# Four graph layers on 128 small graphs: two more columns in the H B^-1 H' matmuls, and the first weights loaded in smaller pieces in another order

## The chip, the core and the metric

The kernel runs on one core of a Trainium2 chip. The metric is the device time of one execution in microseconds (us), where smaller is better. Matmuls run on TensorE (PE in the profile, with its weight loads as PEld), elementwise work on VectorE (DVE), ScalarE (ACT) and GpSimd (POOL). SyncE (SP) issues every DMA, in one queue and in program order.

## What is computed

There are 128 graphs of 64 nodes with 512 features (x), each with a 64x64 weighted adjacency matrix (adj, many entries zero). Four layers follow each other, and each one is `x = layernorm(x + layer(x))`:

```
layer 0:  s = (x @ w0) @ a0;  A = exp(leaky(8*tanh((s_i + s_j)/8))) * adj, rows normalised
          to the sum of adj's row;  out = A @ x @ w0
layer 1:  attention: adj * exp(q k^T), rows normalised, times v   (weights Wq, Wk, Wv)
layer 2:  a graph-wide softmax of q_i . (sum_j adj_ij k_j), times v   (Wqk, Wv)
layer 3:  two hypergraph convolutions with relu and layernorm between them:
          H = (adj != 0);  w = first row of adj
          Dn_i = sum_e H_ie w_e;  Be_e = number of nodes in e
          conv(x, W) = Dn^-1 H Be^-1 H^T (x @ W^T) + b
```

For this case two things matter. The first is the matrix `G = H Be^-1 H^T` (64x64 for each graph), with the sums that go with it: Dn, the number of edges of each node, and the row sums of adj. The second is that layer 1 and layer 2 need only the product of their q and k weights, so the kernel forms `M1 = Wq^T Wk` and `M2` once, at the start.

## The kernel before, in words

**Tiling.** The 8192 nodes are 64 tiles of 128 rows, two graphs in a tile. Two tiles make a group: there are 32 groups (NG), and `run(g)` (line 986) issues all four layers of one. Two groups make a chunk: there are 16 chunks, and `prepare_chunk(c)` (line 680) makes for four tiles at a time what depends on adj alone. All data is float32, and TensorE takes a float32 matmul as two passes, so one matmul of the program is two MATMUL rows in the trace (the transposes are one).

**Products.** A 256x512 by 512x512 product is done by `seven_products` in Strassen-Winograd form, with seven block products in place of eight. The weights stand in DRAM as prepared blocks (b11, t1, b21, ... "w", "v", "3a", "3b") and are streamed for every group into a pool of eight buffers called ring. Group 0 uses the blocks of w0 straight from where they were made (`first_use`); group 1 is the first that reads them back (DMA ring<-w).

**TensorE modes.** Matmuls over all 128 rows and columns are "whole". Work on single graphs runs on 64x64 quarters of the array (mode "quarters"; in the profile 64*64) or on halves of its columns ("columns", 128*64).

**Order of the work.** Nothing is issued in source order. Every operation is recorded with an engine, an estimated cost, a key (its due time) and the buffers it touches. `Order.run` (line 140) then plays a list schedule with these costs, and `choose` (line 122) weighs whether TensorE stays in its mode or turns. The resulting order on each engine is fixed by dependencies ("pinned", line 1153), so the profile has nearly all instructions on one line, L1159, and tiles must be used to tell them apart. A DMA's recorded size sets how long the plan takes the link to be busy; for x and adj, `load` (line 338) records 2*128*1024 bytes in both cases. SP has at most eight DMAs under way: the ninth waits for the first to land.

**Start.** Wq and Wk are loaded in halves of 256 rows with key -12 (lines 418 to 425), then w0, a0, x of group 0 and adj of chunk 0. `gram` (line 553) forms M1: for each of four column blocks c it takes a PSUM bank and adds four steps of k (128 rows of weight each), two steps for each operation. M2 follows from Wqk in the same way. The row dots of w0 with a0 give u0 = w0 a0, from which s comes.

**G of a chunk.** hA is H, bh is H Be^-1 (written by POOL), and w is a small tile of its own (128 x 4 x 2), whose first column ACT fills with the first row of adj and whose second column is one. Line 708 issues the matmuls of a chunk as quarters:

```
quarters_of(N, lambda g: N * g, hA, lambda i: bh.t[:, i])
quarters_of(1, lambda g: P + 3 * g, turned, lambda i: ones)
quarters_of(2, lambda g: P + 3 * g + 1, hA, lambda i: w.t[:, i])
```

Each call is eight matmuls (2 x 2 x 2), with 64, one and two columns. The first gives G, the second the row sums of adj, and the third Dn and the edge counts. The first and the third have the same weights, hA. They write into the same two banks, from which ACT copies G into gm and DVE copies the sums.

Of the kernel before, what the change touches and what calls it, by code (L numbers as in the profile page):

```python
# [16 lines left out]
P = 128  # L17
B, N, D, DH = 128, 64, 512, 1024
T = B * N // P
GT = 2  # L20
# [222 lines left out]
def w_pe(n, times=1):  # L243
    return times * 2 * max(112, n * 27 // 32)
# [15 lines left out]
def kernel(  # L260
# [34 lines left out]
    def kind(name, n, *shape, space=None):  # L295
        kinds[name] = [(space or sbuf).tile([P, *shape], FP, name=f"{name}{i}") for i in range(n)]
# [4 lines left out]
    kind("h", 2, GT, DH)  # L301
    kind("k2", 2, D)
    kind("adj", 10, CT, N)
    kind("kept", 12, CT, N)
    kind("k1", 2, CT, N)
    kind("e", 7, GT, N)
    kind("w", 2, CT, 2)
    kind("col", 40, 16)
    kind("bank", 8, D, space=psum)
    kinds["product"] = [None] * 3  # L310
# [27 lines left out]
    def load(b, src, view=None):  # L338
        dma(2 * P * 1024, [], [b], lambda: view(b.t) if view else b.t, lambda: src)

    NOW = 100.0

# [2 lines left out]
    make_identity(nc, ident)  # L345
    ones = sb("ones", 1)
    nc.vector.memset(ones, 1.0)
    for t_ in kinds["w"]:
        nc.vector.memset(t_, 1.0)
    mhalf = sb("mhalf", GT)  # L350
    nc.vector.memset(mhalf, -0.5)
# [29 lines left out]
    xs, adjs, turned_adjs, prepared = {}, {}, {}, {}  # L381

    def load_x(g):
        order.key = BASE[g] - 6.0 if g else -11.0
        xs[g] = Buf("x", 4)
        load(xs[g], x_g[g])

    def load_adj(c):
        order.key = BASE[GC * c] - 7.0 if c else -10.5
        adjs[c] = Buf("adj")  # L390
        load(adjs[c], adjT[:, ts(c, CT * N)], lambda t_: t_.rearrange("p t i -> p (t i)"))

        turned = turned_adjs[c] = Buf("adj", 2 * GT)
        for t in range(GT):
            for h in range(2):
                dma(P * 256, [], [turned[2 * t + h]],
                    lambda t=t, h=h: turned.t[ts(t, N)].rearrange("p (g h) i -> p g h i", h=2)[:, :, h],
                    lambda t=t, h=h: adjT_c[c, t][:, :, h])
# [16 lines left out]
    def rows_of(b, cols):  # L415
        return b.t.rearrange("p (c o) -> p c o", o=cols)

    order.key = -12.0
    wq1_raw, wk1_raw = [], []
    for h in range(2):  # L420
        for made, w in ((wq1_raw, wq1), (wk1_raw, wk1)):
            b = Buf("k4", 2)
            order.add("SP", 500, [], [b], lambda b=b, h=h, w=w: nc.sync.dma_start(
                out=rows_of(b, D), in_=w.rearrange("(h c p) o -> h p c o", h=2, p=P)[h]), size=4 * P * 1024)
            made.append(b)
    order.key = -11.5
    w0_raw = raw(w0, 2, "ring")
    a0_b = Buf("k2")
    dma(P * 2048, [], [a0_b], lambda: a0_b.t,
        lambda: bass.AP(tensor=a0.tensor, offset=a0.offset, ap=[[0, P], [1, D]]))  # L430
    load_x(0)
    load_adj(0)
    mask_c = plain_in("mask_c", mask, T)
    order.key = -10.0
# [115 lines left out]

    def gram(name, left, right):

        m = const(sb(name, len(USE), 2, D // 2), 2 * len(USE))
        place = {k: i for i, k in enumerate(USE)}
        place["b12"] = place["t3"]

        def emit(ps, c, h):
            for k in (2 * h, 2 * h + 1):  # L560
                nc.tensor.matmul(ps.t, rows_of(left[h], D)[:, k % 2, ts(c, P)], rows_of(right[h], D)[:, k % 2],
                                 start=(k == 0), stop=(k == KC - 1))
# [38 lines left out]


    wqk_h = wqk2.rearrange("(h o) i -> h o i", h=2)
    order.key = -9.5
    wq2_raw, wk2_raw = raw(wqk_h[0], 2), raw(wqk_h[1], 2)
# [74 lines left out]
    def prepare_chunk(c):  # L680
        order.key = BASE[GC * c] - 3.0 if c else 0.5
        adj, turned = adjs[c], turned_adjs[c]
        m = mask_c.t[:, ts(c, CT)]
        hA, bh, am = (Buf("kept") for _ in range(3))
# [12 lines left out]

        ps = [Buf("bank") for _ in range(2)]
        gm, sums = Buf("kept"), Buf("col")

        def quarters_of(n, at, left, right):
            for g in range(CT // 2):
                for h, (cols, _) in enumerate(halves):
                    for t, (rows, _) in enumerate(halves):
                        nc.tensor.matmul(ps[t].t[cols, at(g) : at(g) + n], left.t[rows, 2 * g + h], right(2 * g + h)[rows],
                                         start=True, stop=True)

        def emit_g():
            quarters_of(N, lambda g: N * g, hA, lambda i: bh.t[:, i])
            quarters_of(1, lambda g: P + 3 * g, turned, lambda i: ones)  # L710
            quarters_of(2, lambda g: P + 3 * g + 1, hA, lambda i: w.t[:, i])

        pe(720, [turned, hA, bh, w], [*ps, gm], emit_g, mode="quarters", matmuls=40)
        for t in range(2):
            act(P, [ps[t]], [gm], lambda t=t: nc.scalar.copy(
                gm.t.rearrange("p (g t) i -> p t g i", t=2)[:, t], ps[t].t[:, :P].rearrange("p (g i) -> p g i", i=N)), NOW)
            dve(6, [ps[t]], [sums], lambda t=t: nc.vector.tensor_copy(
                sums.t[:, : 3 * CT].rearrange("p (k g t) -> p t g k", t=2, k=3)[:, t],
                ps[t].t[:, P : P + 6].rearrange("p (g k) -> p g k", k=3)), NOW)
        radj = sums  # L720
        dn, n_edges = (slice(CT * k, CT * (k + 1)) for k in (1, 2))
# [18 lines left out]
        prepared[c] = adj, turned, gm, am, radj, g1, dc, dh  # L740


    KEYS = ("11", "12", "21", "22")
# [242 lines left out]
    def run(g):  # L986
# [3 lines left out]

        step(0)
        xt = xs.pop(g)
        adj, turned, gm, am, radj, g1, dc, dh = prepared[g // GC]
# [29 lines left out]
        seven_products(*left, first_use["w0"] if g == 0 else streamed("w0"), *scaled_into(at_x, radj, own, D // 2))  # L1023
        layer_norm(xt)


# [203 lines left out]
```

## Time and profile before

| | us |
|---|---|
| median of 3 runs | 2177.75 |
| lowest and highest | 2177.24, 2178.48 |
| the profiled execution's own time | 2177.52 |
| its span in the trace (first to last instruction) | 2175.7 |
| TensorE busy in the span | 2153.9 |
| VectorE, ScalarE, GpSimd busy | 1557.7, 856.3, 386.1 |
| moved by DMA | 476.36 MB, mean 219 GB/s |

The span is what the trace covers; the execution's own time has 1.8 us more. The page of the profile gives busy times and the chain of work that ended last. The timeline merges instructions of one kind that follow each other into a row of start, length, what it is and how many; matmuls are pipelined and their ends are modelled, so the cost of a block is read from its start to the start of the next one, not from its length. The view of waits totals the idle time of an engine by what ended it. The view by windows gives the busy time, the granted TensorE clock (PEclk, 1.00 is full) and the DMA rate of a stretch.

### The profile page before, as it was taken

What the parts mean: (1) busy time and instruction counts of PE and PEld (TensorE: products, weight loads), DVE (VectorE), ACT (ScalarE), POOL (GpSimd) and SP (SyncE); (2) the same over time, 40 slices, a digit from 0 to 9 for tenths busy, and PEclk for the clock granted to TensorE, in tenths of its full rate; (3) what the DMA queues carried; (4) which work ended last, traced back from release to release, by engine and by line L of the source; (5) the groups of instructions that cost most, each with busy time, mean ns of one, the idle gap of its engine ahead of it and who ended that gap; (6) DMA issues with size and microseconds to landing.
All of it is one profiled execution on the core that took longest, in us unless ns stands there. A gap on an engine that the chain in (4) does not pass through costs nothing.

```text
span 2175.7 us, 51913 instructions
## 1 busy us (share of the span) xinstructions
PE 2153.9 (99%) x21085; PEld 1720.9 (79%) x21085; DVE 1557.7 (72%) x3967; ACT 856.3 (39%) x1812; POOL 386.1 (18%) x399
## 2 busy tenths in 40 slices
PE   8999999999999999999999999999999999999998
PEld 4887787877887788888878877878887888878866
DVE  5777767677777777777777776777777777766675
ACT  2435343343433433343443434434334333343433
POOL 1113021021201222111222111212012221012120
PEclk9999999999999999999999999999999999999999
DMA  9676668667665667666666666676656666655475
GB/s 299 229 252 242 206 206 280 220 215 238 215 219 198 208 219 236 218 200 207 211 227 218 220 206 206 205 239 216 217 196 213 224 220 223 204 192 204 159 255 196
DMA packets 174302, 476.36 MB, mean 219 GB/s; under 512 B 35760, under 2 KB 45296, under 8 KB 174064
## 3 DMA queue, kind: packets, MB, share of 16 engines
q1 hardware_dynamic: 174064, 473.05, 65.7%
q8 instruction: 166, 2.72, 0.5%
q14 instruction: 72, 0.59, 0.1%
HBM read 443.33 MB, written 29.66 MB: 217 GB/s over the span
## 4 chain that ended last, share of the span: by engine, by line
PE 98%; DMA 1%; DVE 0%; ACT 0%; issue 0%; SPq 0%; DVEq 0%; ACTq 0%
PE bank L1159 98%; DMA ring<-w 0%; DMA x<-in_x_dram 0%; DVE k L1159 0%; DMA k<-in_wk_dram 0%; ACT x L1159 0%; ACT k L1159 0%; DVE col L1159 0%; DVE x L1159 0%; SPq L1159 0%; DVE h L1159 0%; ACT u_b L1159 0%; ACT e L1159 0%; DVEq L1159 0%; ACTq L1159 0%
## 5 line engine op out<-in xcount | busy, mean ns | idle before, releaser
L1159 PE MATMUL bank<-ring,k 128*128 128x256 f32 (+1 forms) x3968 | 1039.9, 410 | 3.0 <-ACT k L1159 1.9
L1159 PEld LDWEIGHTS bank<-ring,k 128*128 128x128 f32 x3968 | 728.3, 190 | 207.2 <-issue 113.7
L1159 ACT COPY k<-bank 128x512 f32<-128x512 f32 (+1 forms) x640 | 304.2, 503 | 646.6 <-PE bank L1159 558.4
L1159 DVE SCALAR_TENSOR_TENSOR x<-bank,col,x 128x256 f32<-128x256 f32 (+1 forms) x832 | 400.3, 500 | 194.0 <-PE bank L1159 183.5
L1159 PEld LDWEIGHTS bank<-k,m 128*128 128x128 f32 x3584 | 428.6, 192 | 29.1 <-issue 17.2
L1159 PE MATMUL bank<-k,m 128*128 128x128 f32 x3584 | 437.8, 275 | 0.6 <-ACT k L1159 0.5
L1159 PE MATMUL bank<-ring,h 128*128 128x256 f32 (+1 forms) x1408 | 412.7, 439 | 0.0
L1159 POOL TENSOR_TENSOR col<-col,mhalf 128x2 f32<-128x2 f32 (+1 forms) x161 | 111.6, 693 | 1462.8 <-DVE col L1159 1171.8
L1159 PEld LDWEIGHTS bank<-ring,h 128*128 128x128 f32 x1408 | 259.1, 190 | 81.5 <-issue 55.0
L1159 DVE TENSOR_TENSOR k<-bank,k 128x256 f32<-128x256 f32 x384 | 154.0, 422 | 142.2 <-PE bank L1159 136.8
L1159 ACT ACTIVATE x<-x,col,col 128x512 f32<-128x512 f32 x256 | 195.9, 810 | 148.7 <-DVE col L1159 146.4
L1159 DVE BATCH_NORM_STATS2 col<-x 128x6 f32<-128x512 f32 x256 | 174.9, 689 | 6.3 <-DVE x L1159 0.5
L1159 DVE SCALAR_TENSOR_TENSOR h<-bank,col,b3a_b 128x512 f32<-128x512 f32 x128 | 95.7, 748 | 63.7 <-PE bank L1159 63.0
L1159 ACT ACTIVATE k<-bank,u_c 128x128 f32<-128x128 f32 x256 | 80.4, 365 | 133.5 <-PE bank L1159 130.2
L1159 DVE TENSOR_TENSOR k<-k 128x256 f32<-128x256 f32 x226 | 107.3, 475 | 32.5 <-ACT k L1159 32.0
L1159 ACT ACTIVATE h<-h 128x512 f32<-128x512 f32 x128 | 80.3, 630 | 110.8 <-DVE h L1159 110.7
L1159 ACT ACTIVATE h<-h,col,col 128x512 f32<-128x512 f32 x128 | 95.6, 805 | 68.1 <-DVE col L1159 68.0
L1159 PEld LDWEIGHTS bank<-k,k 128*64 128x64 f32 (+1 forms) x2112 | 77.6, 140 | 51.7 <-DVE k L1159 24.5
L1159 PE MATMUL bank<-k,k 128*64 128x64 f32 (+1 forms) x2112 | 106.6, 238 | 6.8 <-DMA k<-in_wk_dram 6.2
L1159 DVE SCALAR_TENSOR_TENSOR h<-bank,col,h 128x512 f32<-128x512 f32 x128 | 93.1, 747 | 20.8 <-PE bank L1159 19.6
L1159 POOL TENSOR_TENSOR k<-k,b3b_b 128x512 f32<-128x512 f32 x64 | 81.4, 1271 | 134.0 <-DVE h L1159 65.0
L1159 POOL TENSOR_TENSOR x<-x,bv_b 128x512 f32<-128x512 f32 x64 | 81.2, 1272 | 76.5 <-PE bank L1159 57.6
(98 smaller groups left out, 1511.2 us busy)
## 6 DMA issues: line engine op xcount, KB each, us to landing
ring<-3a SPq DMA_DIRECT2D x224, 512.0 KB, 4.5
ring<-3b SPq DMA_DIRECT2D x224, 512.0 KB, 4.5
ring<-v SPq DMA_DIRECT2D x189, 512.0 KB, 3.9
ring<-w SPq DMA_DIRECT2D x93, 512.0 KB, 3.4
x<-in_x_dram SPq DMA_DIRECT2D x32, 512.0 KB, 4.5
ring<-v SPq DMA_DIRECT2D x63, 256.0 KB, 3.7
out_dram<-x SPq DMA_DIRECT2D x31, 512.0 KB, 3.4
ring<-w SPq DMA_DIRECT2D x31, 256.0 KB, 4.1
```

The costliest lines, as they stand in the source:

```text
L1159: made = f(*args, **kwargs)
```

## The change

In the chunk's matmuls, the two columns of w move into bh, which becomes 66 columns wide. The third call of `quarters_of` is gone; G, Dn and the edge counts come out of one call with 66 columns. A graph's results now lie 67 columns apart in the bank, with the row sum of adj as the last one. The plan's cost of this operation goes from 720 to 400 ns and its count of matmuls from 40 to 16.

At the start, Wq and Wk come in pieces of 128 rows, a0 and the halves of w0 are put between them, then x of group 0; x of group 1 gets an earlier key, and the turned parts of adj of chunk 0 a later one. `gram` takes a number of steps: M1 takes one k at a time over all four banks, M2 two at a time. The sizes that the plan assumes for x and adj are the real ones. The two halves of Wqk are loaded in turn (q, k, q, k). The pool "kept" has nine buffers, with two of the kind bh beside it.

```
-    kind("kept", 12, CT, N)
+    kind("kept", 9, CT, N)
+    kind("bh", 2, CT, N + 2)
-    kind("w", 2, CT, 2)
...
-        order.key = BASE[g] - 6.0 if g else -11.0
+        order.key = (-11.0, -10.3)[g] if g < 2 else BASE[g] - 6.0
-        load(xs[g], x_g[g])
+        load(xs[g], x_g[g], P * GT * D * 4)
...
+        order.key += 0.0 if c else 0.6
...
     order.key = -12.0
-    for h in range(2):
-        for made, w in ((wq1_raw, wq1), (wk1_raw, wk1)):
-            b = Buf("k4", 2)
-            order.add("SP", 500, [], [b], lambda b=b, h=h, w=w: nc.sync.dma_start(
-                out=rows_of(b, D), in_=w.rearrange("(h c p) o -> h p c o", h=2, p=P)[h]), size=4 * P * 1024)
-            made.append(b)
-    order.key = -11.5
-    w0_raw = raw(w0, 2, "ring")
-    a0_b = Buf("k2")
-    dma(P * 2048, [], [a0_b], ...)
-    load_x(0)
+    for k in range(KC):
+        load_rows(wq1_raw, wq1, k)
+        load_rows(wk1_raw, wk1, k)
+        if k == 0:
+            dma(P * 2048, [], [a0_b], ...)
+            load_half(w0_raw, w0, 0)
+        if k == 1:
+            load_half(w0_raw, w0, 1)
+            load_x(0)
+            order.key = -12.0
...
-    def gram(name, left, right):
+    def gram(name, left, right, steps):
...
-        for c in range(KC):
-            ps = Buf("bank")
-            for h in range(2):
-                pe(w_pe(D, KC // 2), [left[h], right[h]], [ps], lambda ps=ps, c=c, h=h: emit(ps, c, h))
+        banks = [Buf("bank") for _ in range(KC)]
+        for ks in (range(i, i + KC // steps) for i in range(0, KC, KC // steps)):
+            for c in range(KC):
+                pe(w_pe(D, len(ks)), [b[k // 2][k % 2] for k in ks for b in (left, right)], [banks[c]],
+                   lambda c=c, ks=ks: emit(banks[c], c, ks))
...
-    m1 = gram("m1", wq1_raw, wk1_raw)
+    m1 = gram("m1", wq1_raw, wk1_raw, KC)
-    m2 = gram("m2", wq2_raw, wk2_raw)
+    m2 = gram("m2", wq2_raw, wk2_raw, KC // 2)
...
-        pool(W, [hA, be], [bh], lambda: nc.gpsimd.tensor_mul(bh.t, hA.t, per_tile(be.t[:, :CT])))
-        w = Buf("w")
-        act(CT, [turned], [w], lambda: nc.scalar.copy(w.t[:, :, 0:1], turned.t[:, :, 0:1]))
+        pool(W, [hA, be], [bh[0]], lambda: nc.gpsimd.tensor_mul(bh.t[:, :, :N], hA.t, per_tile(be.t[:, :CT])))
+        act(CT, [turned], [bh[1]], lambda: nc.scalar.copy(bh.t[:, :, N : N + 1], turned.t[:, :, 0:1]))
...
-            quarters_of(N, lambda g: N * g, hA, lambda i: bh.t[:, i])
-            quarters_of(1, lambda g: P + 3 * g, turned, lambda i: ones)
-            quarters_of(2, lambda g: P + 3 * g + 1, hA, lambda i: w.t[:, i])
-        pe(720, [turned, hA, bh, w], [*ps, gm], emit_g, mode="quarters", matmuls=40)
+            quarters_of(N + 2, lambda g: (N + 3) * g, hA, lambda i: bh.t[:, i])
+            quarters_of(1, lambda g: (N + 3) * g + N + 2, turned, lambda i: ones)
+        pe(400, [turned, hA, bh], [*ps, gm], emit_g, mode="quarters", matmuls=16)
```

More of the change, by code (lines that the diff above doesn't have):

```diff
@@ L336, in dma, with load @@
         order.add("SP", 500, reads, writes, lambda: nc.sync.dma_start(out=out(), in_=in_()), size=size)
-    def load(b, src, view=None):
-        dma(2 * P * 1024, [], [b], lambda: view(b.t) if view else b.t, lambda: src)
+    def load(b, src, size, view=None):
+        dma(size, [], [b], lambda: view(b.t) if view else b.t, lambda: src)
     NOW = 100.0
@@ L347 @@
     nc.vector.memset(ones, 1.0)
-    for t_ in kinds["w"]:
+    for t_ in kinds["bh"]:
         nc.vector.memset(t_, 1.0)
@@ L390, in load_adj @@
         adjs[c] = Buf("adj")
-        load(adjs[c], adjT[:, ts(c, CT * N)], lambda t_: t_.rearrange("p t i -> p (t i)"))
+        load(adjs[c], adjT[:, ts(c, CT * N)], P * CT * N * 4, lambda t_: t_.rearrange("p t i -> p (t i)"))
         turned = turned_adjs[c] = Buf("adj", 2 * GT)
+        order.key += 0.0 if c else 0.6
         for t in range(GT):
@@ L416, in rows_of, with load_rows, load_half @@
         return b.t.rearrange("p (c o) -> p c o", o=cols)
-    order.key = -12.0
-    wq1_raw, wk1_raw = [], []
-    for h in range(2):
-        for made, w in ((wq1_raw, wq1), (wk1_raw, wk1)):
-            b = Buf("k4", 2)
-            order.add("SP", 500, [], [b], lambda b=b, h=h, w=w: nc.sync.dma_start(
-                out=rows_of(b, D), in_=w.rearrange("(h c p) o -> h p c o", h=2, p=P)[h]), size=4 * P * 1024)
-            made.append(b)
-    order.key = -11.5
-    w0_raw = raw(w0, 2, "ring")
-    a0_b = Buf("k2")
-    dma(P * 2048, [], [a0_b], lambda: a0_b.t,
-        lambda: bass.AP(tensor=a0.tensor, offset=a0.offset, ap=[[0, P], [1, D]]))
-    load_x(0)
+    wq1_raw, wk1_raw = ([Buf("k4", 2) for _ in range(2)] for _ in range(2))
+    w0_raw = [Buf("ring", 2) for _ in range(2)]
+    a0_b = Buf("k2")
+    def load_rows(b, w, k):
+        order.add("SP", 500, [], [b[k // 2][k % 2]], lambda: nc.sync.dma_start(
+            out=rows_of(b[k // 2], D)[:, k % 2], in_=w[ts(k, P)]), size=P * D * 4)
+    def load_half(b, w, h):
+        order.add("SP", 500, [], [b[h]], lambda: nc.sync.dma_start(
+            out=rows_of(b[h], D), in_=w.rearrange("(h c p) o -> h p c o", h=2, p=P)[h]), size=P * PIECE * 4)
+    order.key = -12.0
+    for k in range(KC):
+        load_rows(wq1_raw, wq1, k)
+        load_rows(wk1_raw, wk1, k)
+        if k == 0:
+            dma(P * 2048, [], [a0_b], lambda: a0_b.t,
+                lambda: bass.AP(tensor=a0.tensor, offset=a0.offset, ap=[[0, P], [1, D]]))
+            load_half(w0_raw, w0, 0)
[3 more added lines that the diff above has]
+            order.key = -12.0
     load_adj(0)
@@ L557, in gram, with emit @@
         place["b12"] = place["t3"]
-        def emit(ps, c, h):
-            for k in (2 * h, 2 * h + 1):
-                nc.tensor.matmul(ps.t, rows_of(left[h], D)[:, k % 2, ts(c, P)], rows_of(right[h], D)[:, k % 2],
+        def emit(ps, c, ks):
+            for k in ks:
+                nc.tensor.matmul(ps.t, rows_of(left[k // 2], D)[:, k % 2, ts(c, P)], rows_of(right[k // 2], D)[:, k % 2],
                                  start=(k == 0), stop=(k == KC - 1))
+        banks = [Buf("bank") for _ in range(KC)]
[3 more added lines that the diff above has]
+                   lambda c=c, ks=ks: emit(banks[c], c, ks))
         for c in range(KC):
-            ps = Buf("bank")
-            for h in range(2):
-                pe(w_pe(D, KC // 2), [left[h], right[h]], [ps], lambda ps=ps, c=c, h=h: emit(ps, c, h))
+            ps = banks[c]
             for i in range(2):
@@ L603 @@
     wqk_h = wqk2.rearrange("(h o) i -> h o i", h=2)
+    wq2_raw, wk2_raw = ([Buf("k4", 2) for _ in range(2)] for _ in range(2))
     order.key = -9.5
-    wq2_raw, wk2_raw = raw(wqk_h[0], 2), raw(wqk_h[1], 2)
+    for h in range(2):
+        load_half(wq2_raw, wqk_h[0], h)
+        load_half(wk2_raw, wqk_h[1], h)
     order.key = 3.0
-    m2 = gram("m2", wq2_raw, wk2_raw)
+    m2 = gram("m2", wq2_raw, wk2_raw, KC // 2)
     order.key = 6.0
@@ L683, in prepare_chunk @@
         m = mask_c.t[:, ts(c, CT)]
-        hA, bh, am = (Buf("kept") for _ in range(3))
+        hA, bh, am = Buf("kept"), Buf("bh", 2), Buf("kept")
         be = Buf("col")
@@ L708, in emit_g, with per_g @@
         def emit_g():
-            quarters_of(N, lambda g: N * g, hA, lambda i: bh.t[:, i])
-            quarters_of(1, lambda g: P + 3 * g, turned, lambda i: ones)
-            quarters_of(2, lambda g: P + 3 * g + 1, hA, lambda i: w.t[:, i])
-        pe(720, [turned, hA, bh, w], [*ps, gm], emit_g, mode="quarters", matmuls=40)
+            quarters_of(N + 2, lambda g: (N + 3) * g, hA, lambda i: bh.t[:, i])
+            quarters_of(1, lambda g: (N + 3) * g + N + 2, turned, lambda i: ones)
+        pe(400, [turned, hA, bh], [*ps, gm], emit_g, mode="quarters", matmuls=16)
+        def per_g(t):
+            return ps[t].t[:, : CT // 2 * (N + 3)].rearrange("p (g k) -> p g k", k=N + 3)
         for t in range(2):
             act(P, [ps[t]], [gm], lambda t=t: nc.scalar.copy(
-                gm.t.rearrange("p (g t) i -> p t g i", t=2)[:, t], ps[t].t[:, :P].rearrange("p (g i) -> p g i", i=N)), NOW)
+                gm.t.rearrange("p (g t) i -> p t g i", t=2)[:, t], per_g(t)[:, :, :N]), NOW)
             dve(6, [ps[t]], [sums], lambda t=t: nc.vector.tensor_copy(
                 sums.t[:, : 3 * CT].rearrange("p (k g t) -> p t g k", t=2, k=3)[:, t],
-                ps[t].t[:, P : P + 6].rearrange("p (g k) -> p g k", k=3)), NOW)
-        radj = sums
-        dn, n_edges = (slice(CT * k, CT * (k + 1)) for k in (1, 2))
+                per_g(t)[:, :, N:]), NOW)
+        dn, n_edges, radj = (slice(CT * k, CT * (k + 1)) for k in range(3))
         g1, dc, dh = Buf("col"), Buf("col"), Buf("col")
@@ L739, in prepare_chunk @@
         dve(W, [am, mr], [am], lambda: nc.vector.tensor_mul(am.t, am.t, mr.t))
-        prepared[c] = adj, turned, gm, am, radj, g1, dc, dh
+        prepared[c] = adj, turned, gm, am, sums, g1, dc, dh
     KEYS = ("11", "12", "21", "22")
@@ L992, in run @@
         xt = xs.pop(g)
-        adj, turned, gm, am, radj, g1, dc, dh = prepared[g // GC]
+        adj, turned, gm, am, sums, g1, dc, dh = prepared[g // GC]
         own = slice(g % GC * GT, g % GC * GT + GT)
@@ L1022, in run @@
         step(2)
-        seven_products(*left, first_use["w0"] if g == 0 else streamed("w0"), *scaled_into(at_x, radj, own, D // 2))
+        seven_products(*left, first_use["w0"] if g == 0 else streamed("w0"), *scaled_into(
+            at_x, sums, slice(2 * CT + own.start, 2 * CT + own.stop), D // 2))
         layer_norm(xt)
```

## The prediction

> **What bounds the kernel now.** I read the page first, for the engine that ends the span.
>
> ```profile
> span 2175.7 us, 51913 instructions
> PE 2153.9 (99%) x21085; PEld 1720.9 (79%) x21085; DVE 1557.7 (72%) x3967; ACT 856.3 (39%) x1812; POOL 386.1 (18%) x399
> PE 98%; DMA 1%; DVE 0%; ACT 0%; issue 0%; SPq 0%; DVEq 0%; ACTq 0%
> ```
>
> TensorE is busy for 99% of the span, and 98% of the chain that ended last is its own. What it no longer has to do comes off the time; what any other engine is spared does not. The view by windows says where the rest lies (the columns after the length are busy us of PE, PEld, DVE, ACT and POOL, then PEclk, DMA share and GB/s).
>
> ```profile
> 6.16:12.09 5.93, 5.93 (x7) 2.50 (x8) 1.25 (x2) 0.00 (x0) 0.00 (x0) 1.00 1.05 377
> ...
> 59.87:63.29 3.42, 3.42 (x13) 2.89 (x12) 1.20 (x3) 1.60 (x5) 1.27 (x1) 0.50 0.86 243
> ...
> 150.00:2100.00 1950.00, 1948.95 (x19155) 1563.75 (x19155) 1407.39 (x3573) 775.97 (x1629) 347.43 (x353) 1.00 0.65 215
> ```
>
> From 150 us to 2100 us TensorE never rests at a full clock. In the first 5.93 us of its work only 7 passes start, 0.85 us each, though later ones of the same shape start every 0.43 us: about 3 us are lost there. From 59.87 us the clock is granted at 0.50 for 3.42 us, which loses another 1.7 us. The waits of TensorE are few:
>
> ```profile
> PE bank L1159 <- DMA k<-in_wk_dram: 6.2, 1, 6.2
> PE bank L1159 <- ACT k L1159: 2.4, 4, 1.5
> PE bank L1159 <- ACT x L1159: 2.3, 1, 2.3
> PE bank L1159 <- DVE e L1159: 1.1, 1, 1.1
> PE bank L1159 <- DMA ring<-w: 0.9, 2, 0.7
> ```
>
> All but those for ACT k lie in the first 60 us. So the change has two places: the chunk's matmuls, on TensorE all the way through, and the start.
>
> **Part 1: the two columns.** One chunk in TensorE's timeline (start, length, what, count):
>
> ```profile
> 45.51 0.46 PE L1159 MATMUL bank<-kept,kept 64*64 64x64 f32 x16
> 45.79 0.36 PE L1159 MATMUL bank<-ones,adj 64*64 64x1 f32 x16
> 45.99 0.39 PE L1159 MATMUL bank<-w,kept 64*64 64x2 f32 x16
> 46.23 0.43 PE L1159 MATMUL bank<-e,same 64*64 64x128 f32 x4
> ```
>
> From start to start, 16 passes of 64 columns take 0.28 us, 16 of one column 0.20, and 16 of two columns 0.24 with the step to the next block, which remains. I take 0.21 for the block removed. 16 chunks: 3.4 us less. The two added columns cost at most 2/64 of 0.28 us, in 16 chunks 0.14 us. **Net -3.2 us.** The bounds are 0.18 and 0.24 us for each block, so -2.7 to -3.8.
>
> The Trainium skill, page "TensorEngine Tiling (Array Packing)", section "Instruction Overhead", puts about 60 cycles on each matmul and says that a free dimension of 1 costs as much as 60. Taken at 2.4 GHz, that is an estimated 25 ns for each pass, and 256 passes would be 6.4 us. The rows above show 13 to 15 ns for each narrow pass, so the sum goes by them.
>
> The rest of this part is free: ACT's copy of adj's row and POOL's product are made as before, into bh; they write the wider rows with 61% and 82% of their engines' time unused. The two memsets of bh (264 columns, where a 128-column one takes 0.17 us) stand at DVE's start, where DVE is idle until 10.1 us; without this cover they would cost some 0.6 us once. "kept" still serves three chunks (12 buffers of four per chunk, 9 of three). The evictions are the same in number.
>
> **Part 2: turns.** The plan is told a shorter block (400 for 720), and everything after it is chosen anew. In the built orders of the two programs TensorE goes from whole to divided (quarters or columns) 147 times before and 131 after, back as often, and between quarters and columns 66 and 68 times. The price is read from these rows:
>
> ```profile
> 90.09 1.89 PE L1159 MATMUL bank<-ring,k 128*128 128x256 f32 x8
> 91.82 0.38 PE L1159 MATMUL bank<-e,same 128*128 128x128 f32 x2
> ...
> 102.56 1.89 PE L1159 MATMUL bank<-ring,k 128*128 128x256 f32 x8
> 104.38 1.15 PE L1159 MATMUL bank<-k,k 128*64 128x64 f32 x32
> ```
>
> Eight passes followed by a whole block take 1.73 us, followed by a divided one 1.82: 0.09 us to leave. Coming back: 32 passes e,x (35.89 to 36.51) take 0.62 us and 64 of them (79.37 to 80.47) 1.10, each with one return, so 32 cost 0.48 and the return 0.14. 16 pairs at 0.23 are 3.7 us, less two turns between divided forms at 0.13: **-3.4 us**. All other matmuls are the same in kind and number, but for one sum over a graph that is now made in quarters. In this order the last 290 us of TensorE's work are the same in both programs, block for block, so the end (three short waits, then 7.6 us of normalising and storing) stays.
>
> **Part 3: the start.** Before, the first product waited for two loads of 512 KB. The first of these takes 4.0 us from its issue at 0.72, so that 512 KB are there at 4.7 us; after, these are the first pieces of Wq and Wk, and TensorE begins at about 4.85 in place of 6.16. But does that reach the end? Ahead of the first product that needs w0 back from DRAM (group 1's first), the new order has 39.8 us of TensorE work: 27.5 of M1 and M2 (64 passes at 0.43), 6.1 of group 0's products, the rest small blocks. With 1.7 to 3.4 us lost to the half clock at the beginning, TensorE is there at 46.4 to 48. The DMA comes later:
>
> ```profile
> 49.48 6.42 DMA ring<-w
> ```
>
> This row of the chain shows that before, too, the path ran through such a load. The first of these loads is issued at 47.59, behind the stores of w0 and v1. In the new order the same bytes stand ahead of it but x of group 1 (512 KB, 1.3 us at the 383 GB/s of 3 to 13 us), which is moved ahead to a stretch with a gap (13 to 16 us ran at 111 GB/s); there Wqk's first load now also waits for TensorE to be done with Wq's buffer (8 matmuls of M1, at 13.4 to 15.1 us), and everything on SP behind it: bv, the stores, x of group 2. So the issue comes 0 to 1.3 us earlier, at 46.3 to 47.6, and lands 3.4 us later (the median of ring<-w): 49.7 to 51. The second piece follows after 3.4 us, as before. Group 0's normalisation stands on DVE behind the eviction of that first product, as it did at 55.83. Then its transposes, which ended the wait of 2.3 us at 59.40 before, start at 54 to 55.5. Before, 43.2 us of work by the same prices stood ahead of them, so 16.2 us were lost by then; after, it is 42.6, so 11.4 to 12.9 are lost. **The start gains 3.3 to 4.8 us; I take 3.9.** What is late next is the same pair, reload and normalisation.
>
> TensorE now waits 2 to 4 us for the reload, as long as the 2.3 us after which the clock dropped before or longer, so I leave the lost 1.7 us in. The Trainium skill, page "TensorE: Matmul & The Clock Gate", Part 1, has a free-running window of 3.4 us, and one idle window halves the clock. The trace agrees with the length (3.42 us at 0.50, after a wait of only 2.3), and by this rule the longer wait of the new order gives the drop again; were it gone, the sum would be 1.7 us lower.
>
> **The sum.** -3.2 - 3.4 - 3.9 = -10.5 us. Against the profiled execution (2177.52 us: its span of 2175.7 and 1.8 around it) that is 2167.0. The median of the runs shown is 0.2 us above the profiled execution, which I neglect.
>
> **Rivals.**
>
> *The start gives nothing* (20%). The reload lands when it did, the longer wait drops the clock for two windows, and the 3.9 us are gone. For it: DMA is 90% busy over the first 54 us, and more small loads (eight slots under way) can only slow SP. Against: the 2.3 us wait was for the normalisation, which now comes earlier. 2177.5 - 6.6 = 2170.9, and with up to 2 us of loss 2171 to 2173.
>
> *The start gives all* (13%). The reload comes 2 us sooner since the gap at 13 us closes, and the clock does not drop: 3 to 4 us more, 2163 to 2164.
>
> *The columns do not do what they say* (8%). The narrow passes were beside other work, as the overlapping lengths (0.39 us in rows 0.24 apart) might suggest: then 3.2 us are not gained, and the time is 2170. Against it: TensorE's next block starts after the block each time.
>
> *Slower* (6%). One mechanism: SP is one queue, and the order of its DMAs is chosen anew too. In every chunk five loads of adj (3.5 us on SP) stand ahead of weights "3b" for the next product:
>
> ```profile
> 1489.42 3.52 SPq L1159 DMA_DIRECT2D adj<-in_adjT_dram  x5
> 1493.57 5.73 SPq L1159 DMA_DIRECT2D ring<-3b  x4
> ```
>
> The first of these four lands 4.5 us after its issue (the page's median), at 1498.1, and its matmul stands in TensorE's row from 1495.82 at about 1498.5: there is hardly room. A load that comes d later than this room stops TensorE once in each chunk for d, 16 d in all, and from d = 0.66 us on the kernel is no faster; at 1 us it is 2183. Against it: in the new order two of the four now stand ahead of adj, and the last two, by the order, are used some 10 us later.
>
> **How the numbers follow.** My forecast (2165 to 2169) has 53%. About 0.2% (4.4 us) is what a measurement of this kernel can tell from no change: faster is under 2173.4. Faster: 53 + 13, 15 of the 20, 7 of the 8: 88%. Same: 5 of the 20, 1 of the 8, 2 of the 6: 8%. Slower: 4%. The range leaves out the worst of the first rival and the slower one above, and a little below: 2162.5 to 2173.
>
> **What would show it.** Right: the group bank<-w,kept is gone, TensorE's busy time is about 6.5 us lower, the blocks of 66 columns are within 0.02 us of the old 0.28, the first matmul starts at 4.8 to 5, the longest wait at the start is for DMA ring<-w at 47 to 51 us, and the transposes of group 0 start at 54 to 55.5. Wrong: waits of TensorE between 150 and 2100 us; a first matmul after 6 us; or a wait for the reload that ends after 53 us.

## The result

The changed kernel takes 2165.29 us (median of 4, 2164.20 to 2166.22), beside 2177.94 us for the kernel before on the same chip: a ratio of 0.9942 (95% interval 0.9925 to 0.9959), 12.65 us less. The forecast was 2167.0 us, in the range 2162.5 to 2173. The time is near it, but two of its three terms are not: the turns gave more than forecast, and the start gave next to nothing. The experiments below are about these two.

The profiled execution took 2166.22 us. Its page, with TensorE's busy time down by 11.1 us where some 6.5 were forecast:

```profile
span 2164.4 us, 51412 instructions
...
PE 2142.8 (99%) x20831; PEld 1717.2 (79%) x20831; DVE 1541.9 (71%) x3967; ACT 856.9 (40%) x1812; POOL 386.1 (18%) x399
...
PE 97%; DMA 2%; DVE 0%; ACT 0%; SPq 0%; issue 0%; POOL 0%; POOLq 0%; DVEq 0%; ACTq 0%
```

The waits of TensorE (engine, tile and line, what ended the wait: us in total, times, longest). The longest is now one of 4.9 us for a reload of w0; those for ACT x and DVE e are gone:

```profile
PE bank L1178 <- DMA ring<-w: 4.9, 1, 4.9
PE bank L1178 <- DMA k<-in_wk_dram: 4.8, 2, 4.1
PE bank L1178 <- DMA k<-in_wqk_dram: 1.8, 1, 1.8
PE bank L1178 <- ACT k L1178: 1.7, 3, 1.2
```

The view by windows. TensorE is as full in the middle as it was; the clock is granted at 0.50 for 6.83 us, twice as long as before, though the slow passes at the very beginning cost less (4.12 us in place of 5.93). The view prints 1.00 for that first stretch, but only five passes start in its 4.12 us, where later ones take 0.43 us each. How long it lasts differs between executions: in a second trace of this kernel (after_again, below), whose first matmul starts at 4.18, it goes on until 10.02 and not 8.26.

```profile
4.14:8.26 4.12, 4.12 (x5) 1.82 (x6) 0.00 (x0) 0.00 (x0) 0.00 (x0) 1.00 0.79 251
52.63:59.46 6.83, 3.96 (x10) 3.06 (x11) 3.64 (x10) 2.48 (x7) 0.72 (x1) 0.50 0.90 312
150.00:2100.00 1950.00, 1949.73 (x19059) 1566.27 (x19059) 1396.58 (x3592) 780.75 (x1636) 347.76 (x355) 1.00 0.64 216
```

One chunk's matmuls in TensorE's timeline. The block of 66 columns takes 0.28 us from start to start, as that of 64 did, and the third block is gone:

```profile
27.98 0.46 PE L1178 MATMUL bank<-bh,kept 64*64 64x66 f32 x16
28.26 0.36 PE L1178 MATMUL bank<-ones,adj 64*64 64x1 f32 x16
28.55 0.70 PE L1178 MATMUL bank<-k,k 128*128 128x512 f32 x1
```

And the start, in the same view. Group 1's first product on the reloaded w0 (55.02) stands ahead of group 0's transposes (60.52); it waits 4.86 us, and all behind it with it:

```profile
49.02 1.13 PE L1178 MATMUL bank<-ring,k 128*128 128x256 f32 x4
55.02 2.04 PE L1178 MATMUL bank<-ring,k 128*128 128x256 f32 x4 [4.86 <-DMA ring<-w]
56.85 0.63 PE L1178 MATMUL bank<-e,same 128*128 128x128 f32 x2
57.97 2.71 PE L1178 MATMUL bank<-ring,k 128*128 128x256 f32 x8 [0.48 <-DVE k L1178]
60.52 1.04 PE L1178 MATMUL bank<-ident,x 128*128 128x128 f32 x8
```

**How the traces are compared.** All kernels do the same groups, so I take from each trace when the first pass of row_of,e of a group starts on TensorE, and subtract the same of before. Where this difference stands still nothing is won; where it falls by the same in each chunk, the gain lies in every chunk. Up to group 5 the groups are interleaved differently and single values say little.

```
us later (+) or earlier (-) than before, at group   6      12      20      28      31
changed kernel                                  -3.11   -5.83   -8.25  -10.60  -10.60
cols_same_plan                                  +0.15   -0.92   -1.68   -2.34   -2.33
short_plan                                      -0.90   -2.91   -3.97   -5.39   -5.39
cols_only                                       -3.53   -6.24   -8.11  -10.02  -10.02
start_only                                      -4.21   -4.58   -4.58   -4.14   -4.14
w0_twice                                        -4.95   -7.66  -10.22  -12.57  -12.57
x1_late                                         -7.06   -9.77  -11.89  -14.23  -14.23
after_again (the changed kernel once more)      -2.33   -5.04   -7.46   -9.81   -9.82
x1_late_again (x1_late once more)               -6.23   -8.94  -11.50  -12.97  -12.97
```

Each row is one execution. Two traces of the same kernel end 0.8 and 1.3 us apart, so differences of about 1 us between rows say nothing; the rate from group to group, where the clock is full, is the surer number.

The changed kernel gains all the way, some 0.6 us a chunk, and not at the start: group 0's transposes come 1.1 us later than before (60.52, where the first four came at 59.40). From the last group to the end of the span another 0.7 us are won (the span is 11.3 us shorter), which is not followed further.

### The profile page after: what moved, and what is told of

Its sections match the earlier page's. It is cut to its first block, busy times and chain, and to the rows that moved or that the text cites. A ratio compares the mean times of both kernels' runs of the same rounds, so it can differ in the third digit from the quotient of the medians.

```text
span 2164.4 us, 51412 instructions
## 1 busy us (share of the span) xinstructions
PE 2142.8 (99%) x20831; PEld 1717.2 (79%) x20831; DVE 1541.9 (71%) x3967; ACT 856.9 (40%) x1812; POOL 386.1 (18%) x399
## 4 chain that ended last, share of the span: by engine, by line
PE 97%; DMA 2%; DVE 0%; ACT 0%; SPq 0%; issue 0%; POOL 0%; POOLq 0%; DVEq 0%; ACTq 0%
PE bank L1178 97%; DMA x<-in_x_dram 0%; DMA k<-in_wk_dram 0%; DMA ring<-in_wv_dram 0%; DMA k<-in_wqk_dram 0%; DMA v<-ring 0%; DMA ring<-w 0%; SPq L1178 0%; ACT k L1178 0%; DVE k L1178 0%; ACT x L1178 0%; DVE x L1178 0%; DVE col L1178 0%; POOL ring L1178 0%; POOLq L1178 0%
## 5 line engine op out<-in xcount | busy, mean ns | idle before, releaser
L1178 DVE TENSOR_TENSOR k<-k 128x256 f32<-128x256 f32 x226 | 95.8, 425 | 41.0 <-ACT k L1178 40.6
```

Of the source, the lines that this page charges most:

```text
L1178: made = f(*args, **kwargs)
```

## The experiments

**Theory A** at the outset: the start gives nothing, a pair of turns costs 0.33 us and not 0.23, and the columns give 4.6 us. **Theory B**: the three terms are as predicted. Four kernels do one or two of the parts; they ran together, beside 2176.97 us for the kernel before.

**cols_same_plan**: the columns alone, with the plan told the old block. It turns 147 times, as before.

```
-            quarters_of(N, lambda g: N * g, hA, lambda i: bh.t[:, i])
-            quarters_of(1, lambda g: P + 3 * g, turned, lambda i: ones)
-            quarters_of(2, lambda g: P + 3 * g + 1, hA, lambda i: w.t[:, i])
-        pe(720, [turned, hA, bh, w], [*ps, gm], emit_g, mode="quarters", matmuls=40)
+            quarters_of(N + 2, lambda g: (N + 3) * g, hA, lambda i: bh.t[:, i])
+            quarters_of(1, lambda g: (N + 3) * g + N + 2, turned, lambda i: ones)
+        pe(720, [turned, hA, bh], [*ps, gm], emit_g, mode="quarters", matmuls=40)
```

> The before kernel with the two columns in bh alone; the plan is told the old 720 ns and 40 matmuls, and its order has the old 147 turns to divided modes, 147 back. Only the block of a chunk differs. Theory A (the columns and the turns carry the whole gain, and were priced too low; the start gives nothing): the block falls from 0.81 us to some 0.52 (0.24 us of two-column passes with their step, 0.05 less for the 66-column passes than for the 64-column ones, as in the trace of after), so 16 x 0.29 = -4.6 us, 2173.3. Theory B (the prices of the prediction hold and the start gave the rest): -3.2 us, 2174.7.

Measured: 2174.98 us, ratio 0.9986 (0.9977 to 0.9995). By the groups it is 1.13 us behind after the start, where the clock was granted at 0.50 in two stretches (54.69 to 58.10 and 61.51 to 64.93), and then 0.233 us better in each chunk that nothing disturbs: -3.7 in 16 chunks at that rate, -3.46 from group 1 to the end. The price of the columns is nearer to B; that the time is B's, too, owes something to the 1.13 us lost at the start.

**short_plan**: the kernel before, with only the plan told the shorter block. It turns 132 times.

```
-        pe(720, [turned, hA, bh, w], [*ps, gm], emit_g, mode="quarters", matmuls=40)
+        pe(400, [turned, hA, bh, w], [*ps, gm], emit_g, mode="quarters", matmuls=16)
```

> The before kernel with nothing changed but what the plan is told of the chunk's block: 400 ns and 16 matmuls in place of 720 and 40; the three calls stay. Its order has 132 turns to divided modes and 132 back, where before has 147 each. Theory A: a pair of turns costs 0.33 us, because the first whole pass after a divided block holds the next one back by another 0.10 us: 15 x 0.33 = -5.0 us, 2172.9. Theory B: 15 x 0.23 less two turns between divided modes at 0.13: -3.2 us, 2174.7. A third: the order alone gives nothing that lasts (the plan of before is as good): 0.

Measured: 2169.43 us, ratio 0.9961 (0.9949 to 0.9974). In the trace -5.39 us for 15 pairs fewer, 0.36 each; between groups 8 and 28, where a chunk has one pair fewer, -2.09 to -5.39, 0.33 a chunk. Nothing of the computation has changed; only the order has. A is nearer on the price, and the third theory falls. The time is better than A's: 7.5 us under before by the medians, while the profiled execution was the slowest of the five (2171.63 us).

Where the pair's price stands can be read from the rows. A chunk's block of G in this kernel, and then in the kernel before:

```profile
1159.06 1.16 PE L1159 MATMUL bank<-kept,h 64*64 64x64 f32 x64
1160.04 0.41 PE L1159 MATMUL bank<-kept,kept 64*64 64x64 f32 x16
1160.27 0.36 PE L1159 MATMUL bank<-ones,adj 64*64 64x1 f32 x16
```

```profile
1198.10 1.15 PE L1159 MATMUL bank<-k,k 128*64 128x64 f32 x32
1199.18 0.46 PE L1159 MATMUL bank<-kept,kept 64*64 64x64 f32 x16
1199.46 0.36 PE L1159 MATMUL bank<-ones,adj 64*64 64x1 f32 x16
```

Behind other quarters the 16 passes of G take 0.23 us, behind columns 0.28: 0.05 to enter the quarters. And 64 passes take 0.98 us ahead of more quarters (kept,h above), where they take 1.09 to 1.10 ahead of a whole block: 0.11 to return. With the prediction's 0.09 to leave and A's 0.10 behind the return (in turns_2's rows below) a pair is 0.35.

**cols_only**: both of these, on the old start.

```
-        pe(720, [turned, hA, bh], [*ps, gm], emit_g, mode="quarters", matmuls=40)
+        pe(400, [turned, hA, bh], [*ps, gm], emit_g, mode="quarters", matmuls=16)
```

> The before kernel with the columns and the short plan, the start as before: 132 turns each way. Theory A: -4.6 - 5.0 = -9.6 us, 2168.3, within 3 us of the changed kernel. Theory B: -6.4 us, 2171.5, with 6 us missing to the changed kernel.

Measured: 2166.36 us, ratio 0.9948 (0.9935 to 0.9960), and -10.02 us in the trace. Where nothing disturbs, a chunk is 0.645 us shorter: 0.233 of the columns and 0.41 of the order. This is nearly the whole gain of the changed kernel, without its start, and more than either theory. Some 0.9 us of it are the execution's: the same loads and the same M1, but four passes at the slow rate in place of six, so that the 21st pass starts at 16.87 where it started at 17.76 in before. At 50 to 62 us products that wait for the reload stand ahead of group 0's transposes, as in the changed kernel:

```profile
54.70 3.51 PE L1159 MATMUL bank<-ring,k 128*128 128x256 f32 x8 [1.94 <-DMA ring<-w]
61.72 1.04 PE L1159 MATMUL bank<-ident,x 128*128 128x128 f32 x8
```

**start_only**: the changed kernel with the old three blocks and the plan told 720 and 40.

```
-            quarters_of(N + 2, lambda g: (N + 3) * g, hA, lambda i: bh.t[:, i])
-            quarters_of(1, lambda g: (N + 3) * g + N + 2, turned, lambda i: ones)
-        pe(400, [turned, hA, bh], [*ps, gm], emit_g, mode="quarters", matmuls=16)
+            quarters_of(N, lambda g: N * g, hA, lambda i: bh.t[:, i])
+            quarters_of(1, lambda g: P + 3 * g, turned, lambda i: ones)
+            quarters_of(2, lambda g: P + 3 * g + 1, hA, lambda i: w.t[:, i])
+        pe(720, [turned, hA, bh, w], [*ps, gm], emit_g, mode="quarters", matmuls=40)
```

> The before kernel with the new loads, the new steps of M1 and M2 and the new sizes in the plan, and the chunk's three calls as before (146 turns each way). Theory A: the first matmul is 2 us earlier, the half clock of the beginning shorter or the same, but the wait for the reload of w0 is longer and the clock drops after it: 0, within 1.5 us either way, 2176.5 to 2179. Theory B: -3.9 us and up to -6: 2172 to 2174. A third theory, that the sizes told to the plan spare TensorE something in every group: the gain grows from group to group between 150 and 2100 us, 0.2 us a chunk.

Measured: 2172.27 us, ratio 0.9976 (0.9966 to 0.9986): 4.7 us under before by the medians, -4.03 us at group 0, and between -4.0 and -4.6 from there to the end. That is the 3.9 us of the prediction; A's "the start gives nothing" falls, and so does the third theory, since the gain does not grow. Its timeline:

```profile
48.86 0.43 PE L1178 MATMUL bank<-e,same 64*64 64x128 f32 x4
51.80 1.93 PE L1178 MATMUL bank<-e,x 64*64 64x64 f32 x64 [2.51 <-DVE e L1178]
53.65 1.89 PE L1178 MATMUL bank<-ident,x 128*128 128x128 f32 x8
55.38 1.89 PE L1178 MATMUL bank<-ring,k 128*128 128x256 f32 x8
```

The transposes (ident,x) start at 53.65, and the products that need the reload follow at 55.38 without a wait. So the parts alone make -10.02 and -4.14, together -14.2, and the changed kernel has -10.6. A new theory A: the start's 4 us are lost by the order of TensorE's work at 50 to 60 us, a product that waits for the reload ahead of the transposes. Its rival: loads and normalisation end late in the new order, whatever stands ahead. Four more kernels, again run together (before: 2177.49 us).

**w0_twice**: group 1 uses w0's blocks where they were made, so that the first reload is wanted a group later.

```
-        seven_products(*left, first_use["w0"] if g == 0 else streamed("w0"), *scaled_into(
+        seven_products(*left, first_use["w0"] if g < 2 else streamed("w0"), *scaled_into(
```

> The changed kernel, but group 1's first products use w0's blocks where group 0 left them, so that the reload of w0 is wanted only from group 2 on. Theory A: in the changed kernel the start's 4 us are lost because a product that waits 4.86 us for the reload stands on TensorE ahead of group 0's transposes (until 55.02). Then no wait for the DMA of ring<-w is left before 60 us, the transposes of group 0 start at 54 to 56 in place of 60.5, and the time is 3 to 5 us under the changed kernel's 2165.3: 2160.3 to 2162.3. Theory B: the start gives nothing because the loads and group 0's own normalisation end no sooner in the new order: the transposes stay at 59 to 61 and the time at 2164.5 to 2166.

Measured: 2163.57 us (2163.11 to 2164.24), ratio 0.9938 (0.9925 to 0.9950). The time is between the two, and the transposes come where B has them, not at 54 to 56:

```profile
47.50 4.09 PE L1178 MATMUL bank<-ring,k 128*128 128x256 f32 x16
54.77 0.49 PE L1178 MATMUL bank<-e,same 128*128 128x128 f32 x2 [3.17 <-ACT e L1178]
55.09 5.30 PE L1178 MATMUL bank<-ring,k 128*128 128x256 f32 x16
```

The wait for the reload is gone, and one for ACT takes its place: 3.17 us until group 1's e is there, and 16 passes of group 1's products still stand ahead of the transposes (60.23). Taking away what the early product waited for is worth 2 us; it is not the whole.

**x1_late**: the reload stays, and x of group 1 is loaded at its old place.

```
-        order.key = (-11.0, -10.3)[g] if g < 2 else BASE[g] - 6.0
+        order.key = BASE[g] - 6.0 if g else -11.0
```

> The changed kernel, but x of group 1 keeps its old, later place in SP's order. In the built order the transposes of group 0 then stand ahead of group 1's first product on the reloaded w0, and the reload stays. Theory A (that order is what costs the 4 us): the transposes start at 53 to 56, the wait for the reload is under 2.5 us, and the time is 2161 to 2163 (133 turns for 131 take 0.7 us back). Theory B (DMA and normalisation are late in any case, or the later x makes group 1 late by as much): 2164.5 to 2167.

Measured: 2162.15 us (2160.32 to 2164.11), ratio 0.9932 (0.9918 to 0.9945). The group view has -14.23, near the sum of cols_only and start_only. In its timeline the transposes start at 50.34, ten us before those of the changed kernel and sooner than A said, and the products with the reload follow at 55.27 without a wait:

```profile
46.95 0.36 PE L1178 MATMUL bank<-ones,adj 64*64 64x1 f32 x16
49.45 0.44 PE L1178 MATMUL bank<-e,same 64*64 64x128 f32 x4 [2.15 <-DVE col L1178]
50.34 1.36 PE L1178 MATMUL bank<-ident,x 128*128 128x128 f32 x8 [0.45 <-ACT x L1178]
51.63 1.86 PE L1178 MATMUL bank<-e,x 64*64 64x64 f32 x64
53.42 2.02 PE L1178 MATMUL bank<-k,m 128*128 128x128 f32 x8
55.27 2.75 PE L1178 MATMUL bank<-ring,k 128*128 128x256 f32 x12
```

The reload is hardly earlier here. SP's rows of its first piece, in this kernel and then in the changed one:

```profile
49.99 0.54 SPq L1178 DMA_DIRECT2D ring<-w  x1
```

```profile
50.21 0.54 SPq L1178 DMA_DIRECT2D ring<-w  x1
```

It lands at 53.97 here and at 54.88 there. What differs is what TensorE does meanwhile: transposes, e,x and k,m fill the time until 55.27. That speaks for A and against the rival. By the view of waits TensorE waits 10.8 us in all in this kernel and 14.2 in the changed one.

One thing besides the order differs: the wait of 1.8 us for Wqk at 24 us, which the changed kernel has, is gone, since Wqk's loads no longer wait for x of group 1 to land. It does not decide, for start_only has this wait too (1.5 us), its transposes stand ahead as well, and its 4 us are there.

**a0_late**: a0 is loaded behind w0's second half and not as the third DMA, where it takes 6.05 us from issue to landing.

```
         if k == 0:
-            dma(P * 2048, [], [a0_b], ...)
             load_half(w0_raw, w0, 0)
         if k == 1:
             load_half(w0_raw, w0, 1)
+            dma(P * 2048, [], [a0_b], ...)
```

> The changed kernel, but a0 is loaded behind w0's second half and not as the third DMA, where it takes 6.05 us and the transfers of 4 to 6 us run at 115 GB/s. Theory C: that slow load delays wq and wk and by them all of the start; without it the M1 products run through sooner, the reload is issued 1 to 2 us earlier and the time is 2163 to 2164.5. Theory A (only the order around the reload counts, and here one product on the reloaded w0 still stands ahead of the transposes): 2164.5 to 2167, with a wait for ring<-w of 3 us or more.

Measured: 2166.79 us (2164.45 to 2168.07), ratio 0.9952 (0.9939 to 0.9964). No gain: C falls. A's time is right, not its number: the longest wait for the reload is 1.8 us, but 1.92 us for DVE e precede it, the clock is granted at 0.50 for 10.2 us, and the transposes start at 61.16, again behind products of group 1.

**cols_w0_twice**: cols_only with the edit of w0_twice.

> The kernel with the two columns and the short plan on the old start (2166.4), but group 1 uses w0's blocks in place. Theory A: there the reload ended no long wait ahead of the transposes, so that little is to be had: 2164.5 to 2166.5. Theory B (the reload costs in every start): the same 3 to 5 us as for the changed kernel, 2161.4 to 2163.4.

Measured: 2166.97 us (2165.77 to 2168.09), ratio 0.9954 (0.9941 to 0.9966); cols_only had 2166.36. That is nearest to A, 0.5 us above its range: in the old start taking the reload away gains nothing that can be measured. It does not show that the wait was free. cols_only waited 1.9 us for the reload; here TensorE waits 2.5 us for ACT e, as it does in w0_twice.

**after_again and x1_late_again**: the changed kernel and x1_late side by side.

> The changed kernel once more, beside the one with x of group 1 in its old place, on one chip. Theory A (the start's 4 us are lost by the order around the reload): it stays at 2164 to 2166.5 and its trace shows the wait of 4 to 5 us for ring<-w and the transposes at 60 to 61 again. Theory B (the loss was an accident of one execution): the wait is under 3 us in this trace.

> The changed kernel with x of group 1 in its old place in SP's order, once more, on the chip of the run before. Theory A: 3 to 4 us under the changed kernel on this chip, transposes of group 0 at 49 to 52 and no wait for ring<-w over 1 us. Theory B: within 1.5 us of the changed kernel.

Measured: 2166.12 us (2165.56 to 2166.93) and 2161.87 us (2160.86 to 2163.40), 4.25 us apart, and 0.9929 of before (0.9916 to 0.9941) for the second. The wait for ring<-w is 4.5 us in the first, with the transposes at 61.31; in the second they are at 50.46. Theory A holds in both, with 61.31 and 4.25 us just outside its numbers. In the second the clock was granted at 0.50 for 6.8 us and in x1_late for 3.4, so the number of these stretches is not what sets the kernels apart.

**turns_2 and turns_8**: the price of a turn, measured by itself. Each product with v2 is two matmuls for each of its seven blocks; between them two (or eight) matmuls in quarters go into a free column of the same bank, so that the products with v2 are lost and the rest of the work stays as it is. The plan is not told, so the order stays. "Passes" in the two expectations are matmuls of the program, each two MATMUL rows in the trace.

```
                         nc.tensor.matmul(o[:, :width], l[:, k, :], b[:, k, :], start=start and k == 0,
                                          stop=k == chunks - 1, skip_group_check=True)
+                        for _ in range(1 if k == 0 and a.get("turn") else 0):
+                            for rows, _ in halves:
+                                nc.tensor.matmul(o[rows, D - 1 : D], same[rows, rows], ones[rows],
+                                                 start=True, stop=True, skip_group_check=True)
```

> The changed kernel with the price of a turn taken by itself: into each of the seven products with v2 of every group, between its two whole passes, two passes in quarters (64x64, one column, into an unused column of the same bank) are put, 224 more pairs of turns, with the plan told nothing. Theory A, a pair of turns costs 0.33 us, since the first whole pass after a return starts 0.10 us late as well: with two passes of some 0.015 us it is 0.36 us each, 81 us in all, a time of 2246. Theory B, the 0.23 us of the prediction: 0.26 us each, 58 us in all, 2223.

> The same with eight passes in quarters in each place. The difference to the kernel with two is six passes, 224 times: at 0.013 to 0.015 us a pass 17 to 20 us more, by either theory; what is left when eight passes are taken off is the turn. If a pass behind a turn costs much more than 0.015 us (a weight load that nothing hides), the difference shows it and the price of the turn goes down by that.

Measured: 2256.20 us and 2334.64 us. Over the changed kernel's 2165.29 that is 90.9 and 169.4 us, 0.406 and 0.756 us in each of 224 places; both expectations for turns_2 are too low, A's by less. The reason is in the second kernel: six more matmuls cost 0.350 us, 0.058 each, not 0.015. Taken off, 0.406 less two of them leaves 0.29 us for the pair of turns. In turns_2's timeline:

```profile
499.39 0.28 PE L1182 MATMUL bank<-ones,same 64*64 64x1 f32 x4
499.60 1.13 PE L1182 MATMUL bank<-ring,k 128*128 128x256 f32 x4
500.66 0.28 PE L1182 MATMUL bank<-ones,same 64*64 64x1 f32 x4
500.87 1.35 PE L1182 MATMUL bank<-ring,k 128*128 128x256 f32 x5
```

From 499.60 to 500.66 stand four whole passes, which take 4 x 0.216 = 0.86 us where nothing turns; the 0.20 more are 0.09 for leaving and 0.10 for the first pass after the return, which holds back the second. The prediction saw the first of these and not the last. The rest of the price lies in the 0.21 us of the narrow rows, which by 0.058 for each of their two matmuls would be 0.12.

## Why the prediction was right, and where it was not

**Part 1, the columns: right in mechanism and size.** -3.2 was forecast (bounds -2.7 to -3.8); by cols_same_plan it is -3.5 to -3.7. The 66 columns cost nothing that shows, where 0.14 us was set aside. The overlapping lengths did not hide the narrow passes.

**Part 2, the turns: right in mechanism, too small in size.** The step that fails is "the return 0.14", and so 0.23 for a pair. It was read from blocks e,x of 32 and 64 passes, start to start, up to the first whole pass. As far as it goes it is about right (0.05 to enter and 0.11 to return), but that view ends where the rest of the price begins: the whole block behind a return is 0.10 us longer than its passes. Measured: 0.29 us for a pair by itself, 0.33 to 0.36 in place, so that the term is -5.4 (short_plan) and not -3.4. In undisturbed chunks it is 0.41. With all blocks between groups 10 and 12 summed by kind, in before and in short_plan, 0.35 of this are the pair, and 0.05 stand in a row of eight products behind k,m that takes 1.78 us in before, where such rows take 1.73; why was not traced. The 0.13 that the prediction put on a turn between divided forms no row shows; the nearest are the 0.05 above. The Trainium skill, page "TensorEngine Tiling (Array Packing)", section "Key Properties", says that a change of tiling mode drains TensorE; it names no price. The runs show one, 0.29 us; that it is a drain they do not show.

**Part 3, the start: the number right alone, but not by its path, and wrong in the whole.** "The start gains 3.3 to 4.8 us; I take 3.9" is what start_only has (-4.03). But there, too, the reload is late: it is issued at 49.50 and lands at 52.95, and the transposes stand ahead of the products that need it. The prediction had them wait behind a reload that lands at 49.7 to 51, so that its number came out is luck. In the changed kernel two steps of it fail. First, "the issue comes 0 to 1.3 us earlier, at 46.3 to 47.6": it came at 50.21, 2.6 us later than before, and landed at 54.88. There the chain of work that ended last runs through a store of v1:

```profile
35.28 6.92 DMA ring<-in_wv_dram
42.35 0.10 issue
42.45 1.70 POOL ring L1178
44.16 5.33 DMA v<-ring
49.51 0.59 SPq L1178
50.21 4.67 DMA ring<-w
```

The store waited for POOL, whose block waited for a load that took 6.92 us, and SP's issue of the last load ahead of the reload waited for the store to land at 49.5. But this is not why the reload is late as such: in x1_late and start_only no store of v1 waits for POOL, and the reload is issued at 49.99 and 49.50. What the three kernels have in common is that SP is late long before. Its rows in the changed kernel, and then in the kernel before:

```profile
25.99 3.36 SPq L1178 DMA_DIRECT2D mask_rows<-e  x1
29.39 5.08 SPq L1178 DMA_DIRECT2D w<-ring  x7
```

```profile
21.13 4.16 SPq L1159 DMA_DIRECT2D mask_rows<-e  x1
25.33 3.69 SPq L1159 DMA_DIRECT2D w<-ring  x6
```

Ahead of the first store of w0 SP waits for ACT, by the view of waits: until 29.12 here, 28.23 in start_only and 27.07 in x1_late, where ACT copies chunk 0's G, and until 24.72 in before, where it writes u0. The prediction counted the bytes ahead of the reload and the wait for Wq's buffer, and not that SP waits for ACT. Second: "what is late next is the same pair, reload and normalisation". The prediction knew that the normalisation stands on DVE behind the eviction of that first product; it took the order as it was and put a price on the DMA alone. In x1_late the reload lands at 53.97, three us after the forecast's 51, and the 4 us are there all the same, since the transposes stand ahead. So the order does it without an earlier reload; what an earlier reload would give in the order of the changed kernel, no run shows (w0_twice, which waits for no reload, won 2 us, and a wait for ACT took its place). That order is the old one: before and cols_only have it, with products that wait for the reload from 54.66 and 54.70 on and transposes at 59.40 and 61.72. An early x does not settle it: start_only has the early x and its transposes first. It is the plan's choice in the whole program.

**The sum.** -3.2 - 3.4 - 3.9 = -10.5 was forecast. By the parts the columns and the order of the short plan give -10.0 together (cols_only; separately -3.5 and -5.4, and of the other 1.2 us some 0.9 are the slow passes at the beginning that this execution was spared). The start adds -0.6 by the changed kernel's first trace and +0.2 by its second, which is nothing that these traces can tell. So the time is right because 2.5 to 3.4 us too little for the turns and columns and 3.3 to 4.1 us too much for the start cancel, and that is luck. The clues the prediction gave did tell them apart: the busy time fell by 11.1 and not 6.5, and the wait for the reload ended at 55.02, after the 53 that it named as wrong. The first matmul started at 4.14, sooner than the 4.8 to 5 it named, and that did not reach the end either. The rival "the start gives nothing" (2171 to 2173) was nearest to what the start did, with a longer wait and two windows of half clock as it said; its time was too high, since it took the other two terms at 6.6 us.

**The slower rival** did not happen: between 150 and 2100 us TensorE is busy for 1949.73 us, so no wait for weights "3b" repeats.

**A version that beats both** is x1_late, the changed kernel with group 1's x where it was: 2161.87 us beside 2166.12.

**Left open**: differences of 0.1 to 0.9 us that come and go at single chunks (cols_only at groups 14 and 21), which were not traced to a wait; what an earlier reload would give in the order of the changed kernel; and what the plan weighs when it puts group 1's product first.

## What to carry to other kernels

Where an engine is full, its order is part of its work: read what a change of mode costs up to the second instruction behind the return, and multiply it by the turns of the built order. Where an engine's queue is fixed, don't only ask when a transfer lands, but what stands behind the instruction that waits for it, and whether work that is ready could stand ahead. And let a sum that comes out right be checked term by term: here two errors of some 3 us cancelled.

## What the runs showed that I had not expected

- A one-column matmul of 64x64 costs 0.058 us when only two quarters are in use (six more in turns_8, 0.350 us). The 16 passes of ones,adj in four quarters take 0.20 us, 0.013 each. The starts of the single passes in the trace show why: with four quarters in use four passes start 7 ns apart, and the next four 58 ns after the first of them; in turns_8 it is two passes, and the next two again 58 ns later. This step is the same for one column, two, 64 and 66. So the prediction's 13 to 15 ns were not the price of a pass but a fourth of that of four side by side, and a narrow pass in quarters costs as much as a wide one. The Trainium skill, page "TensorEngine Tiling (Array Packing)", section "Instruction Overhead", puts about 60 cycles on a matmul, an estimated 25 ns at 2.4 GHz; the step in one quarter is here over twice that, and what sets it no run shows.
- In the first 70 us the clock at 0.50 comes in stretches of 3.4 us or whole multiples: 3.41 us in start_only, 6.83 in the changed kernel, 10.2 in a0_late. The Trainium skill, page "TensorE: Matmul & The Clock Gate", Part 1, has a free-running window of that length. The runs agree with the length, and that it runs on its own fits the two traces of the changed kernel, whose first matmuls start at 4.14 and 4.18 and whose slow first passes end at 8.26 and 10.02.
- a0, one row of DRAM spread over 128 partitions, took 6.05 us as the third DMA (1.63 to 7.68), while the first two, of 256 KB each, took 2.66 and 2.85; moved behind w0 it made nothing faster.
